# Handing out the experts of layer 0 unit by unit, with later stores and later transposes in the scan

## The chip, the cores and the metric

The kernel runs on one core of one Trainium2 chip. Five engines work side by side: TensorE (PE, matmuls; PEld is its weight load), VectorE (DVE), ScalarE (ACT), GpSimd (POOL) and SyncE (SP, which issues nearly all DMAs here). Each takes its instructions in the order of its own queue. The metric is the device time of one execution in microseconds (us). Before the change it is 3905.21 us, the median of three runs (3901.26 to 3909.09).

## The reference: what is computed

Input `x` has 16 sequences of 512 tokens, 128 wide; everything is float32. Two layers follow each other; each normalises `x` and adds an attention branch and a feed-forward branch to it.

```python
xn = _layernorm(x)
x = x + _L0_attn_ref(xn, ...) + _L0_ffn_ref(xn, ...)
xn = _layernorm(x)
x = x + _L1_attn_ref(xn, ...) + _L1_ffn_ref(xn, ...)
```

- `_L0_attn_ref` is a memory that is trained while it reads: a scan over 8 chunks of 64 tokens (all sequences at once). Each step projects keys and values, runs a two-layer network on the keys, takes the gradient of a squared error by hand, clips it and updates the weights. Then every token is read out through the final memory.
- `_L0_ffn_ref` is a convolution over time, attention with 16 heads of 8 (no mask), a layer norm, then a dense mixture of 8 experts: every token goes through every expert (128 to 512 to 128), weighted by a softmax gate, and another layer norm.
- `_L1_attn_ref` is causal attention with 16 heads, a convolution over its result, and a second causal attention with the queries that come out of it.
- `_L1_ffn_ref` picks 8 of 32 experts for each token, with room for 128 tokens in each expert, gathers the tokens, runs the experts and scatters the results.

## The kernel before

**Turns.** The program is not written engine by engine. Work is a set of Python generators ("stages"), and class `Turns` (L269 to L300) steps all that are live once a turn, in order of a priority: 0 the maxima (`tops`, which calls `largest`), 1 the weighted values (`back`, which calls `weighted`), 2 to 5 everything else, 6 the experts of layer 0 (`experts0`, which calls `ffn(b)` for one sequence after the other). PE's instructions keep exactly the order in which the generators write them; the other engines' queues are ordered by a scheduler. `idle(n)` lets n turns pass, `after(...)` waits for a mark, `room()` for a free buffer of `work`. A stage is given with the turn at which it may begin; those of layer 1 begin at fixed turns, from `t0 = 480` in steps of 44 for each sequence (L1456 to L1470), once the scan is over.

**Attention.** For one group of heads, `largest` (L370) writes scores into the PSUM tile `s1` (tag `p1`, one buffer), 1024 columns in a turn, and VectorE takes their maximum into `nm`: one reduction at L395 without a mask, at L387 with one (two instructions), or L394 and L395 for the narrow ones. The width of the causal scores runs through 512, 384, 256 and 128 columns. `weighted` (L419) writes the scores again, transposed, into `s2` (tag `p2`, one buffer); ScalarE takes the exponential into `e` (L466); with a mask POOL clears the upper triangle (L470). The sums over values, `pc`, follow eight heads a turn (up to four in a group at once), in turns in which `tail` (L444) puts "values" among the locks.

**Experts of layer 0.** `ffn(b)` (L526) has 64 units for a sequence: `first(i)` multiplies 128 of the 512 hidden columns of one expert (`phe`, L579) and lets ScalarE take ReLU (L581); `second(i)` multiplies back into `pye` (L591) and, after each fourth, scales by the gate on ScalarE (L598) and adds on POOL (L599). How many units a turn gets is an account. `load_ns` sums an estimate of PE's work in the turn; `credit` grows by `TURN` (2750) less that, up to 4000, and each unit costs 1000. With `pools["pairs"]` true only pairs are handed out, and in a turn with "values" none unless more than three would be:

```python
            credit[0] = min(credit[0] + TURN - load_ns[0], 4000)
            more = int(max(credit[0] + 500, 0) // 1000)
            if pools["pairs"]:
                more = more // 2 * 2 if "values" not in locks or more > 3 else 0
```

`turn4` (L240) writes four transposes and adds 900 to `load_ns` and `array_ns`. `fill` (L194) adds an unused matmul at a turn's end when the experts have been away for more than two turns and `array_ns` is under `ARRAY` (860).

**The scan** (`scan`, L762) runs beside layer 0's attention. A step's keys are transposed into `kT`, `hidden(q)` multiplies and takes SiLU (ScalarE `sg` L848, VectorE `h` L851, POOL `ds` L853 to L855), `hidden_turned` transposes `h` to `hT`, `gradient` multiplies it (`py`) and works out the error; `timed` (L754) gives each part the turn of the step at which it starts (L923 to L928). After eight steps `readout(b)` runs for each sequence and stores `y` (L1034).

**Stores on SP.** SP's queue takes DMAs in order and each waits there for its data. POOL's rows are stored at L1034 (`y` of the readout), L1116 (`x1` after `post0`'s layer norm), L1170 (`x2` in `middle`) and L1279 (`x2` in `last`). The same queue carries the loads of queries and keys (L364), of expert weights (L512, L516) and the maxima's way through memory (L412, L416).

## Time and profile before

| what | before |
|---|---|
| median of three runs | 3905.21 us |
| the profiled execution | 3907.05 us |
| its span | 3905.3 us |
| granted clock of TensorE, mean | 0.961 |
| turns written | 1275 |
| SP's waits for POOL at the stores L1034, L1170, L1116 | 146.6, 115.6, 105.6 us |

The span runs from the first instruction to the last. A row of instructions in the trace has start and duration in us, engine, line and operation, and what it writes and reads; in brackets the idle time before it and what ended it. `xN` is the number of instructions merged. A PE row is the matmul itself; `PEld` rows are weight loads, which overlap with it. A row of a table of windows has the stretch and its length, then for PE, PEld, DVE, ACT and POOL the busy time in us with the number of instructions, then the granted clock of TensorE (1.00 is full speed), the share of the DMA engines and GB/s.

### The profile page before, as it was taken

To read this page: it belongs to the slowest core of one execution; us is meant where nothing else is said; L and a number is where in the kernel's file an instruction comes from. 1 tells how busy PE (TensorE), PEld (TensorE's weight loads), DVE (VectorE), ACT (ScalarE), POOL (GpSimd) and SP (SyncE) were. 2 spreads that over 40 slices of the span, in tenths; PEclk is the share of its full clock that TensorE was granted. 3 is DMA by queue.
4 is the path that set the end of the run, shared out by engine and by line. 5 is a ranking of instruction groups with operands and counts; after the bars stand their busy time and mean duration, and the time that the engine had idled before them with its cause. 6 is when DMAs were issued, how large, how long until landed. Compare 5 with 4: busy or idle time off the path is not lost.

```text
span 3905.3 us, 61944 instructions
## 1 busy us (share of the span) xinstructions
PE 3452.3 (88%) x22265; PEld 1887.3 (48%) x22265; DVE 2325.2 (60%) x5027; ACT 2156.1 (55%) x3687; POOL 1578.2 (40%) x2522
## 2 busy tenths in 40 slices
PE   5999789889889899999998998899999999987877
PEld 2445445445444444555555555555555555533343
DVE  5666556565665555554565666566656666677762
ACT  1555555556566677665555565555555555543443
POOL 5432433344232555324244334433443344333664
PEclk7999899999999999999999999999999999997999
DMA  4222212222222233423443434343434434333343
GB/s 159 65 65 73 64 48 79 71 65 67 81 66 86 85 105 95 149 76 96 128 110 92 122 111 120 95 114 109 121 90 118 113 105 106 105 95 84 85 92 84
DMA packets 289940, 370.52 MB, mean 95 GB/s; under 512 B 46008, under 2 KB 141408, under 8 KB 289248
## 3 DMA queue, kind: packets, MB, share of 16 engines
q1 hardware_dynamic: 282464, 359.73, 32.1%
q0 software_dynamic: 7168, 6.82, 1.1%
q8 instruction: 177, 2.90, 0.3%
q14 instruction: 131, 1.07, 0.1%
HBM read 236.59 MB, written 133.25 MB: 95 GB/s over the span
## 4 chain that ended last, share of the span: by engine, by line
PE 67%; DVE 15%; POOL 6%; ACT 5%; issue 4%; DMA 3%; SPq 1%; POOLq 0%; ACTq 0%; DVEq 0%
PE s L192 17%; PE pye L591 12%; PE pc L192 11%; PE phe L192 11%; DVE nm L395 6%; DVE s L387 3%; PE tp L244 2%; DVE s L394 2%; PE pgr L192 2%; ACT e L466 2%; PE tpc L244 1%; PE pq L192 1%; PE pcv L192 1%; PE pj L192 1%; ACT sq L258 1%
## 5 line engine op out<-in xcount | busy, mean ns | idle before, releaser
L466 ACT ACTIVATE e<-s 128x1024 f32<-128x1024 f32 (+1 forms) x1216 | 1190.9, 979 | 697.0 <-PE s L192 616.6
L395 DVE TENSOR_REDUCE nm<-s 128x2 f32<-128x1024 f32 (+1 forms) x704 | 861.4, 1224 | 645.3 <-PE s L192 638.0
L387 DVE CUSTOM_DVE_ANT_0 s<-s,sb_const 128x512 f32<-128x512 f32 (+1 forms) x1024 | 646.7, 632 | 531.2 <-PE s L192 513.5
L470 POOL TENSOR_SCALAR_AFFINE_SELECT e<-e 128x128 f32<-128x128 f32 (+2 forms) x1408 | 468.8, 369 | 999.5 <-ACT e L466 997.2
L192 PE MATMUL s<-kx,qx 64*128 64x512 f32 (+3 forms) x3072 | 623.7, 432 | 274.3 <-DVE nm L395 145.1
L192 PEld LDWEIGHTS s<-kx,qx 64*128 64x128 f32 x3072 | 276.2, 188 | 913.1 <-issue 338.0
L192 PE MATMUL pc<-e,vp 128*32 128x512 f32 (+3 forms) x6144 | 658.9, 518 | 33.4 <-POOL e L470 33.2
L591 PEld LDWEIGHTS pye<-ew,hTe 128*128 128x128 f32 x4096 | 509.9, 193 | 148.1 <-issue 135.5
L581 ACT ACTIVATE hTe<-phe,sb_cols 128x512 f32<-128x512 f32 x512 | 354.0, 691 | 403.0 <-PE phe L192 401.2
L591 PE MATMUL pye<-ew,hTe 128*128 128x128 f32 x4096 | 575.5, 284 | 0.7 <-DVE vp L345 0.7
L192 PE MATMUL phe<-x1T,ew 128*128 128x512 f32 x1024 | 535.3, 607 | 3.2 <-DVE pr L545 1.0
L192 PE MATMUL s<-qx,kx 64*128 64x512 f32 (+3 forms) x3072 | 508.9, 356 | 31.5 <-ACT e L466 26.9
L192 PEld LDWEIGHTS s<-qx,kx 64*128 64x128 f32 x3072 | 288.1, 189 | 69.7 <-ACT e L466 56.0
L394 DVE TENSOR_TENSOR s<-s,sb_const 128x512 f32<-128x512 f32 (+1 forms) x192 | 168.4, 877 | 244.5 <-PE s L192 244.0
L599 POOL TENSOR_TENSOR ac<-ac,y 128x512 f32<-128x512 f32 x128 | 165.0, 1289 | 338.7 <-ACT y L598 337.9
L192 PEld LDWEIGHTS pc<-e,vp 128*32 128x32 f32 x6144 | 153.4, 111 | 275.9 <-issue 184.7
L598 ACT ACTIVATE y<-pye,pr 128x128 f32<-128x128 f32 x512 | 146.8, 368 | 40.7 <-PE pye L591 36.3
L192 PEld LDWEIGHTS phe<-x1T,ew 128*128 128x128 f32 x1024 | 158.9, 195 | 19.6 <-issue 10.4
L387 DVE DVE_READ_ACCUMULATOR2_ANT nm<- 128x1 f32 x1024 | 144.5, 141 | 0.0
L199 PE MATMUL fill<-sb_pb,sb_const 128*128 128x512 f32 (+2 forms) x236 | 118.4, 590 | 10.3 <-DMA sb_pb<-in_pb 10.2
L205 POOL TENSOR_SCALAR rs_t<-ss 128x4 f32<-128x4 f32 (+1 forms) x56 | 12.5, 223 | 245.5 <-ACT sq L258 244.5
L966 POOL TENSOR_TENSOR cl<-cl,phalf 128x1 f32<-128x1 f32 x8 | 4.5, 568 | 172.9 <-ACT cl L965 172.9
(291 smaller groups left out, 3885.5 us busy)
## 6 DMA issues: line engine op xcount, KB each, us to landing
ew<-in_ew SPq DMA_DIRECT2D x256, 256.0 KB
kx<-rk SPq DMA_DIRECT2D x192, 256.0 KB
qx<-rq SPq DMA_DIRECT2D x128, 256.0 KB
rq<-hi SPq DMA_DIRECT2D x64, 256.0 KB
rq<-lo SPq DMA_DIRECT2D x64, 256.0 KB
rk<-hi SPq DMA_DIRECT2D x64, 256.0 KB
rk<-lo SPq DMA_DIRECT2D x64, 256.0 KB
qx<-r SPq DMA_DIRECT2D x64, 256.0 KB
```

The lines of the kernel that those rows point to most:

```text
L192: nc.tensor.matmul(o, lhsT=lhsT, rhs=rhs, start=start, stop=stop)
L199: nc.tensor.matmul(o[:, 0:n], lhsT=ident, rhs=cell[0][:, 0:n], start=True, stop=True)
L244: nc.tensor.transpose(tp[:, t * P : (t + 1) * P], src(t), ident)
L387: newest[0] = nc.vector.tensor_tensor_reduce(out=sv[:, r, 0, :], in0=sv[:, r, 0, :], in1=row["caus"][:, S - n :], scale=1.0, scalar=-BIG, ...
L394: nc.vector.tensor_tensor(dg, dg, bc(bc(row["caus"][:, S - P :], 1, per), 1, 2), ALU.add)
L395: newest[0] = nc.vector.tensor_reduce(nm[:, qt, :, t : t + per], sv, AX.X, ALU.max)
L466: nc.scalar.activation(e[:, :, 0 : per * n], s[:, :, 0 : per * n], AF.Exp, scale=SCALE)
L470: cleared[0] = nc.gpsimd.affine_select(out=ev[:, r, :, 0:P], in_=ev[:, r, :, 0:P], pattern=[[0, per], [1, P]], compare_op=ALU.is_ge, fill= ...
L581: nc.scalar.activation(hs[i], ph, AF.Relu, bias=col("fb", i))
L591: nc.tensor.matmul(pye[0][:, t, :], lhsT=h[:, t * P : (t + 1) * P], rhs=w2[e][:, f, :], start=(f == 0 and t == 0), stop=(f == 3), skip_gro ...
L598: nc.scalar.mul(y[:, t, :], pye[0][:, t, :], pr[:, t, e : e + 1])
L599: nc.gpsimd.tensor_tensor(ac, ac, y, ALU.add)
```

## The change

Six things are done.

1. `pools["pairs"]` is false in both places where it was true. Units go out singly, in turns with "values" too.
2. Each turn of `largest` sets `look_ns` to a time for its maxima, by width and mask. If the account is not under -2000, the turn gets at least enough units that `load_ns` comes near `look_ns`. It is set to zero at each turn's end.
3. `turn4` adds 600 instead of 900.
4. In the scan, `hidden_turned` and `gradient` start one turn later in each step.
5. The stores of the readout, of `post0` and of `middle` come three, four and three turns after POOL's last instruction. In `post0` and `middle` these idle turns stood behind the store before.
6. The store in `last` comes two turns after POOL's addition.

```diff
-        load_ns[0] += 900
-        array_ns[0] += 900
+        load_ns[0] += 600
+        array_ns[0] += 600
...
-                load_ns[0] = 0.0
+                load_ns[0] = look_ns[0] = 0.0
...
+            look_ns[0] = {S: 2050, 3 * P: 1800, 2 * P: 2450, P: 3000}[n] if causal else 1750
...
+            if credit[0] > -2000:
+
+                more = max(more, int((look_ns[0] - load_ns[0] - 400) / 1000 + 0.7))
...
-    pools.update(ps=ps, p1=1, p2=1, work=3, weights=[att], heads=4, pairs=True)
+    pools.update(ps=ps, p1=1, p2=1, work=3, weights=[att], heads=4, pairs=False)
...
-                *[(4 + 2 * q + i, hidden_turned(q, i)) for q in range(2) for i in range(2)],
-                (7, gradient(0)), (9, gradient(1)),
+                *[(5 + 2 * q + i, hidden_turned(q, i)) for q in range(2) for i in range(2)],
+                (8, gradient(0)), (10, gradient(1)),
...
             nc.gpsimd.tensor_tensor(y, y, xb, ALU.add)
+            yield from idle(3)
             nc.sync.dma_start(acc_b[b], y)
...
         yield from layernorm(x1, x1, row["g1"], row["b1n"])
+        yield from idle(4)
         nc.sync.dma_start(x1d[0, b], flat(x1))
-        yield from idle(4)
...
-    pools["pairs"] = True
+    pools["pairs"] = False
...
         nc.gpsimd.tensor_tensor(x2, x2, xa, ALU.add)
+        yield from idle(3)
         nc.sync.dma_start(acc_b[b], x2)
-        yield from idle(3)
...
             nc.gpsimd.tensor_tensor(x2, x2, xo, ALU.add)
+            yield from idle(2)
             nc.sync.dma_start(acc_b[b], x2)
```

More of the change, by code (lines that the diff above doesn't have):

```diff
@@ L180, in flat @@
         return ap.rearrange("p t d -> p (t d)")
-    load_ns, array_ns, at_ffn = [0.0], [0.0], [-9]
+    load_ns, look_ns, array_ns, at_ffn = [0.0], [0.0], [0.0], [-9]
     def mm(o, lhsT, rhs, start=True, stop=True):
```

## The prediction

> **What bounds the kernel.** I read the page's busy shares first, then its slices, then who waits for whom, stage by stage.

> ```profile
> PE 3452.3 (88%) x22265; PEld 1887.3 (48%) x22265; DVE 2325.2 (60%) x5027; ACT 2156.1 (55%) x3687; POOL 1578.2 (40%) x2522
> PE   5999789889889899999998998899999999987877
> PEclk7999899999999999999999999999999999997999
> ```

> TensorE (PE) is busy 88%, no other engine over 60%, so its work sets the time, except that 453 us of the span are PE idle. The question is who ends those waits. First the scan's stretch (110 to 1570 us), then the causal stretch with experts (1640 to 3260 us), each for the matmuls (PE) and for their weight loads (PEld):

> ```profile
> PE s L192 <- DVE nm L395: 52.7, 60, 3.7
> PE s L192 <- DMA kx<-rk: 14.5, 2, 12.9
> PE tp L244 <- DVE h L851: 6.3, 4, 2.4
> PEld s L192 <- DVE nm L395: 167.0, 167, 4.6
> ...
> PEld s L192 <- DVE nm L387: 147.6, 196, 1.9
> ```

> The columns are total us, times, longest. The score matmul `s` of the maxima waits for VectorE to finish the maximum of the turn before: `p1` has one buffer, so PE may not write the next scores earlier. So a turn has two lower bounds: PE's own work W, and a floor D, first scores to maxima read. I cut the trace's matmuls at each turn's first matmul, by the order that the turn loop writes. Turns without other work show D: 1.82 us for the full maxima without mask, and in layer 1 2.17, 1.82, 2.65 and 3.30 us for widths 512, 384, 256 and 128. W is summed from start-to-start times. An expert unit is about 0.92 us, as here (pye to phe 0.97, phe to the next s 0.96):

> ```profile
> 2403.87 1.14 PE L591 MATMUL pye<-ew,hTe 128*128 128x128 f32 x8
> 2404.84 1.02 PE L192 MATMUL phe<-x1T,ew 128*128 128x512 f32 x2
> 2405.80 0.50 PE L192 MATMUL s<-kx,qx 64*128 64x512 f32 x2
> ```

> The longer of W and D, turn by turn, gives 1533 us for turns 520 to 1050; the trace has 1588, a ratio of 1.036. The rule holds there. For turns 60 to 492 (scan beside layer 0) it gives 1276 where the trace has 1402: 126 us are waits on chains of the scan and on DMAs.

> **The change, part by part.** All sums are against the profiled execution: 3907.05 us with a span of 3905.3. The median of the three runs, 3905.21, is the same within 0.05%.

> *Units one by one, in value turns too, and the bound from the maxima.* Before, in turns 520 to 1050, 253 turns have no unit, 213 two, 64 four. Of the empty ones 180 carry values and last 2.51 us at a W of 1.98; the 73 others last 2.63 at 1.78. Two units last 2.96 at a W of 2.81, four 4.76 at 4.62. The loss, D over W, is in the empty turns: 144 us of 530 turns (1533 less a W of 1389). Following the changed code's loop: 110 empty turns (mean of the longer bound 2.59), 73 with one unit and no values (2.66), 89 with one and values (2.82), 194 with two and no values (2.79), 30 with two and values (3.51), 33 with three (3.54), one of 4.79: 1498 us, of which 1417 are W (28 more because more units are done). Times 1.036: 1552, so **-36**. Ends: -116 (all floors gone: 1417 + 55) and +2: the 128 groups of ScalarE multiplications behind pye (L598, 1.14 us for four at 2405.04) come in more turns ahead of an exponential, and 0.3 us each gives 38 back. I take -36, nearest the turns measured.

> *A transpose counted 600 instead of 900.* Four transposes are 4 x 0.109 us start to start, so either is high. Seven sets per batch of 44 turns give 2100 ns of credit, 2.1 units: the last unit falls in turn 1050 instead of 1104. Turns 1050 to 1105 took 161.8 us. Without experts they go as turns 1105 to 1165 do, 2.53 each: 55 x 2.53 = 139, **-23**; turns 492 to 520 by the rule -2. [...] These windows start after the last expert:

> ```profile
> 3259.00:3418.00 159.00, 144.30 (x1071) 84.55 (x1070) 100.69 (x261) 91.41 (x144) 67.70 (x141) 0.99 0.39 107
> 3418.00:3470.00 52.00, 42.28 (x302) 21.16 (x298) 39.63 (x110) 24.15 (x31) 20.84 (x52) 0.90 0.34 103
> 3470.00:3520.00 50.00, 41.97 (x280) 18.49 (x280) 33.82 (x90) 21.51 (x26) 14.55 (x42) 0.97 0.39 97
> ```

> The clock (third from the end) goes from 0.99 to 0.90. [...]

> *More units during the scan.* Turns 60 to 492 now do 276 units, not 236: W up by 36, the longer bound from 1276 to 1288, since idle time takes most of it: **+12** (ends 0 and +36).

> *Stores later on SP's queue.* One stall shows what they do:

> ```profile
> 443.12 0.50 PE L192 MATMUL s<-qx,kx 64*128 64x512 f32 x2
> ...
> 453.89 0.32 SPq L1116 DMA_DIRECT2D x1d<-x  x1
> 454.39 0.32 SPq L364 DMA_DIRECT2D kx<-rk  x1
> ...
> 457.55 0.76 PE L192 MATMUL s<-kx,qx 64*128 64x512 f32 x1 [12.93 <-DMA kx<-rk]
> ...
> 461.00 2.07 PE L591 MATMUL pye<-ew,hTe 128*128 128x128 f32 x8
> ```

> The store of `x1` stands in SP until POOL's layer norm is done; the keys behind it land late, and PE stands for 13 us. It then runs cold: pye 2.07 instead of 1.14. That turn and the next are 12.5 and 5.0 over their bounds. [...] With four idle turns (13 us) first, the keys go ahead; POOL is next, and the longest store wait was 16.2 (L1116, 105.6 us in 11 waits). The other stores (L1034 146.6, L1170 115.6 us of SP waits) hold nothing that PE waits for beyond some 10 us of DMA waits in layer 1. **-18** (ends 0 and -27). Nothing needs a moved store soon: its readers wait for marks set later.

> *The scan's transposes and gradients a turn later.* PE waits for `h` (L851) at transposes and neighbours 6.3 + 3.9 + 2.4 + 1.7, and for `hT` 5.8: 20 in all. A turn of about 3 us covers most: **-12** (ends -20 and +10). Each of eight steps gets longer; `scan` ends in turn 492 instead of 486. The layer 1 work is dated by turn and absorbs most, but the last attention slips two turns (1275 turns to 1277): 2 x 2.94 = **+6**.

> *POOL bursts.* A layer norm of post0 takes 7 us of POOL (446.33 to 453.87). At 684.8 one, with the scan's keys and `ds`, held ScalarE's `sg`, and the exponential behind it cost PE 8.1 us. By the turn loop post0 and the hidden stage met once before and meet two or three times after (turns 172 to 177, 210 to 218, 338 to 343): **+10** (0 to +20).

> *Fills*: 53 more (170 for 117), nearly all in the first 60 turns or after the experts, where PE waits anyway: 0 (-5 to +10).

> Sum: -36 -23 -2 +12 -18 -12 +6 +10 = **-63**: a span of 3842, 3843 us by the median.

> **Rivals.**
> - *More is won in the scan.* If half of the 126 us of waits there go, instead of the 30 I count, it is 33 more, with more evened floors about 3800. For: most start at a transpose or a store that is moved. Against: several are POOL's own chain, which stays.
> - *Given back.* ScalarE's multiplications and ReLUs, now in value turns, delay the exponentials and cost the 38; with two more POOL meetings (+20) that leaves -5: 3900. For: the exponential is the other single-buffered wait (`p2`). Against: ScalarE is 55% busy.
> - *Slower.* In the scan's stretch experts fill the slack of the turns, so POOL's meeting with `ds` holds `sg`, then the exponential, then PE, each time some 10 us with the cold clock. It decides from eight such meetings over those counted (+80): 3922. For: 126 us of such waits already stand there. Against: only 14 post0 and 8 scan steps share these turns.
> - *The change does nothing*: excluded; empty turns fall from 864 of 1275 to 668 of 1277.

> **How the numbers follow.** Forecast 0.60 (own range 3815 to 3875), more won 0.14, given back 0.09, slower 0.17. The range 3795 to 3915 leaves a tail at each side. 0.2% (8 us) is about what a measurement here tells from no change. Faster by more: 0.60 and 0.14 and a fifth of the given back, 0.76; the same 0.06; slower 0.18.

> **What would show it.** Right: waits of `s` on `nm` in 1640 to 3260 us fall by a third; no 13 us gap behind L1116's store; the last pye some 200 us earlier (before: turn 1104, 3418 us); the stretch behind it at 2.5 us a turn. Wrong: the causal turns no shorter than 2.95 on average with `e` waits in place of `nm`; or the scan's stretch over 1420 us with `ds` and `sg` ahead of PE's gaps.

## The result, and the profile after

The changed kernel takes 3876.49 us (median of five runs, 3871.43 to 3883.21) against 3906.45 us of the kernel before on the same chip: 30 us less, ratio 0.9923 with a 95% interval of 0.9906 to 0.9940. I forecast 3843, which is 63 us less in span. The direction came as forecast; the size is under half. The time lies just outside the 3815 to 3875 that I gave the forecast itself, and inside the whole range of 3795 to 3915.

The page of the changed kernel, busy shares and slices:

```profile
span 3878.0 us, 62191 instructions
PE 3507.0 (90%) x22371; PEld 1934.8 (50%) x22371; DVE 2313.0 (60%) x5027; ACT 2158.5 (56%) x3687; POOL 1573.3 (41%) x2522
PE   6989999889989988989999999999999998888877
PEclk7999999999999999999999999999999999997998
```

PE idles 371 us of the span instead of 453. About 44 us of the 55 us that PE is busier are unused fill matmuls (342 rows of 563 ns for 236 rows before). The slices behind the last expert (from the 34th on) begin two slices earlier than before, and show 8 where the experts gave 9.

Who waits for whom in the changed kernel, the scan's stretch (110 to 1570 us) for PE and PEld, and the causal stretch with experts (1640 to 3240 us) for PEld; the columns are total us, times, longest:

```profile
PE s L192 <- DVE nm L397: 34.2, 35, 5.3
PE phe L192 <- DVE h L856: 12.6, 3, 7.4
PEld s L192 <- DVE nm L397: 103.0, 116, 5.5
...
PEld s L192 <- DVE nm L389: 69.5, 88, 1.9
PEld phe L192 <- issue: 47.6, 151, 0.7
```

The waits for the maxima fall from 52.7 to 34.2, from 167.0 to 103.0 and from 147.6 to 69.5 us. Two waits are new or grew. An expert's `phe` waits for the scan's `h`, and in the causal stretch the weight load of `phe` loses 47.6 us in 151 places to "issue", where before it lost 6.5 us in 19.

I cut the trace after the change at the same turns as before. "Rule" is the sum of the longer of PE's work and the floor of the maxima, with the durations of the prediction; "over" is what the trace has beyond it. The differences are those of the two profiled executions, whose spans are 27 us apart.

| turns | before: us, over | after: us, over | difference | forecast |
|---|---|---|---|---|
| 0 to 60 | 176.3, 38.5 | 172.7, 36.8 | -3.6 | 0 |
| 60 to 492 (scan) | 1401.6, 125.7 | 1401.4, 113.3 | -0.2 | -8 |
| 492 to 520 | 80.5, -0.7 | 79.0, 0.3 | -1.5 | -2 |
| 520 to 1050 (causal, experts) | 1587.9, 55.0 | 1574.9, 76.5 | -13.0 | -36 |
| 1050 to 1105 | 161.8, 3.3 | 140.5, 11.1 | -21.3 | -23 |
| 1105 to the end | 474.5, 77.8 | 487.1, 84.2 | +12.6 | +6 |

Of the 36 us that are missing, 23 lie in turns 520 to 1050, 7.8 in the scan's stretch and 6.6 at the end; the others give 1.4 back.

### The profile page after: what moved, and what is told of

It reads as the page before. It is cut to its first block, busy times and chain, and to the rows that moved or that the text cites. A ratio compares the mean times of both kernels' runs of the same rounds, so it can differ in the third digit from the quotient of the medians.

```text
span 3878.0 us, 62191 instructions
## 1 busy us (share of the span) xinstructions
PE 3507.0 (90%) x22371; PEld 1934.8 (50%) x22371; DVE 2313.0 (60%) x5027; ACT 2158.5 (56%) x3687; POOL 1573.3 (41%) x2522
## 5 line engine op out<-in xcount | busy, mean ns | idle before, releaser
L192 PE MATMUL s<-kx,qx 64*128 64x512 f32 (+3 forms) x3072 | 623.9, 433 | 177.9 <-DVE nm L397 94.1
L192 PE MATMUL pc<-e,vp 128*32 128x512 f32 (+3 forms) x6144 | 652.5, 512 | 28.8 <-POOL e L472 28.5
L192 PEld LDWEIGHTS s<-kx,qx 64*128 64x128 f32 x3072 | 277.0, 190 | 700.0 <-issue 222.1
L593 PEld LDWEIGHTS pye<-ew,hTe 128*128 128x128 f32 x4096 | 520.3, 194 | 196.6 <-issue 181.4
L192 PE MATMUL phe<-x1T,ew 128*128 128x512 f32 x1024 | 559.8, 631 | 21.2 <-DVE h L856 12.6
L192 PE MATMUL s<-qx,kx 64*128 64x512 f32 (+3 forms) x3072 | 507.6, 356 | 25.6 <-ACT e L468 19.4
L192 PEld LDWEIGHTS s<-qx,kx 64*128 64x128 f32 x3072 | 289.7, 190 | 53.8 <-ACT e L468 37.8
L192 PEld LDWEIGHTS pc<-e,vp 128*32 128x32 f32 x6144 | 153.8, 111 | 268.5 <-issue 184.7
L192 PEld LDWEIGHTS phe<-x1T,ew 128*128 128x128 f32 x1024 | 160.0, 195 | 119.2 <-issue 87.2
L199 PE MATMUL fill<-sb_pb,sb_const 128*128 128x512 f32 (+2 forms) x342 | 162.3, 563 | 10.7 <-DMA zrow<-zero 10.2
L199 PEld LDWEIGHTS fill<-sb_pb,sb_const 128*128 128x128 f32 x342 | 57.3, 209 | 56.4 <-issue 41.6
```

The lines of the kernel that those rows point to most:

```text
L192: nc.tensor.matmul(o, lhsT=lhsT, rhs=rhs, start=start, stop=stop)
L199: nc.tensor.matmul(o[:, 0:n], lhsT=ident, rhs=cell[0][:, 0:n], start=True, stop=True)
L593: nc.tensor.matmul(pye[0][:, t, :], lhsT=h[:, t * P : (t + 1) * P], rhs=w2[e][:, f, :], start=(f == 0 and t == 0), stop=(f == 3), skip_gro ...
```

## Experiments

Each ran 4 to 17 times beside the kernel before; "ratio" is to it. Three theories of the gain are set against each other in what was expected: "turns" (it comes from turns in which the floor of the maxima is over PE's work), "early end" (it comes from counting transposes at 600, which ends the experts earlier) and "stalls" (single stalls of the scan's stretch come or go).

| run | what it is | median us | ratio, 95% interval |
|---|---|---|---|
| only_units | before, single units | 3837.84 | 0.9817, 0.9804 to 0.9831 |
| only_600 | before, transposes counted 600 | 3868.14 | 0.9908, 0.9895 to 0.9922 |
| only_stores | before, later stores | 3912.31 | 1.0005, 0.9998 to 1.0013 |
| only_scan | before, scan's turns later | 3874.98 | 0.9915, 0.9901 to 0.9928 |
| after_even | after, no lone unit beside values | 3890.29 | 0.9955, 0.9941 to 0.9969 |
| after_no_scan | after, scan's turns as before; computes wrong values | 3846.79 | 0.9852, 0.9838 to 0.9866 |
| after_no_600 | after, transposes counted 900 | 3854.62 | 0.9867, 0.9853 to 0.9882 |
| after_sg3 | after, three buffers for sg | 3841.23 | 0.9834, 0.9821 to 0.9847 |
| before_sg3 | before, three buffers for sg | 3873.31 | 0.9929, 0.9916 to 0.9942 |
| before_store_on_pool | before, L1116 on POOL's queue | 3894.02 | 0.9973, 0.9964 to 0.9983 |
| after_no_600_sg3 | both of the above, on after | 3821.00 | 0.9786, 0.9773 to 0.9799 |
| units_bound_sg3 | single units, bound, three buffers | 3794.50 | 0.9721, 0.9709 to 0.9734 |

The parts do not add: single units alone win 71 us, 600 alone 41, the scan's turns alone 34, and all together 30. Their stretches tell why (us, and over the rule in brackets):

| run | turns 60 to 492 | 520 to 1050 | 1050 to 1105 | 1105 to the end |
|---|---|---|---|---|
| before | 1402 (126) | 1588 (55) | 162 | 475 |
| after | 1401 (113) | 1575 (76) | 141 | 487 |
| only_units | 1361 (90) | 1563 (65) | 154 | 479 |
| only_600 | 1371 (79) | 1593 (57) | 146 | 476 |
| only_scan | 1344 (71) | 1602 (74) | 165 | 493 |
| after_even | 1394 (108) | 1592 (58) | 140 | 487 |
| after_no_scan | 1398 | 1553 | 137 | 476 |
| after_no_600 | 1362 (109) | 1573 (86) | 157 | 487 |
| after_sg3 | 1370 (82) | 1575 (76) | 138 | 483 |
| before_sg3 | 1373 (97) | 1584 (51) | 162 | 478 |
| after_no_600_sg3 | 1331 (77) | 1572 (85) | 159 | 486 |
| units_bound_sg3 | 1335 (72) | 1552 (61) | 154 | 478 |

### Single units alone

```diff
-    pools.update(ps=ps, p1=1, p2=1, work=3, weights=[att], heads=4, pairs=True)
+    pools.update(ps=ps, p1=1, p2=1, work=3, weights=[att], heads=4, pairs=False)
...
-    pools["pairs"] = True
+    pools["pairs"] = False
```

> The kernel before with single units alone (pairs off in both places; nothing else). Turns theory (the gain comes from turns in which the floor of the maxima is over TensorE's work): by the rule (longer of work and floor) turns 520 to 1050 fall from 1533 to 1498 and the whole by 50 us; less some 25 to 30 us for 114 turns in which a lone unit stands beside values at 0.27 us over the sum: 15 to 30 us faster, ratio 0.992 to 0.996, with turns 520 to 1050 about 10 to 15 us shorter. Early-end theory (the gain comes from counting transposes at 600, which ends the experts 54 turns earlier): within 8 us of before, since here they end only 15 turns earlier. Stalls theory (the gain is single stalls of the scan's stretch that come or go): turns 520 to 1050 unchanged, turns 60 to 492 off by 10 us or more either way.

It is 71 us faster, more than any theory had. Turns 520 to 1050 lose 25 us, where the turns theory gave 10 to 15 and the two others nothing or little. So evening out the units is what pays in the causal stretch. Another 41 us are in the scan's stretch, and 35 of them are not in the rule but over it (126 to 90): stalls, the third theory.

### Lone units beside values

In the changed kernel's trace, 89 turns of the causal stretch have one unit and values. They last 3.09 us where the rule had 2.82: 24 us in all. In `only_units` 102 such turns are 28 us over. Their median is 0.15 us over; no other kind with more than five turns has a median above 0.09. First a turn with values and no unit in the kernel before, then one with a lone `phe` in the changed kernel, PE's matmuls in order of time (start, duration):

```profile
2253.60 0.44 PE L192 MATMUL s<-kx,qx 64*128 64x384 f32 x2
2253.88 0.56 PE L192 MATMUL s<-qx,kx 64*128 64x128 f32 x8
2254.36 1.07 PE L192 MATMUL pc<-e,vp 128*32 128x256 f32 x16
2255.42 0.44 PE L192 MATMUL s<-kx,qx 64*128 64x384 f32 x2
```

```profile
2317.58 0.44 PE L192 MATMUL s<-kx,qx 64*128 64x384 f32 x2
2317.86 0.56 PE L192 MATMUL s<-qx,kx 64*128 64x128 f32 x8
2318.35 1.07 PE L192 MATMUL pc<-e,vp 128*32 128x256 f32 x16
2319.35 1.13 PE L192 MATMUL phe<-x1T,ew 128*128 128x512 f32 x2
2320.41 0.44 PE L192 MATMUL s<-kx,qx 64*128 64x384 f32 x2
```

and the weight load of that `phe`, among the PEld rows:

```profile
2319.35 0.30 PEld L192 LDWEIGHTS phe<-x1T,ew 128*128 128x128 f32 x2 [0.41 <-issue]
```

The first turn is 1.82 us, the floor, and hides what is in it: 0.28 and 0.49 us of scores and 1.00 of `pc`, 1.77 together, for which the rule had 1.60. The second shows it, because `phe` starts only 1.00 us after `pc`. Its weights are loaded only as it starts (0.41 us of waiting), and the unit takes 1.06 us start to start, not the 0.97 and 0.96 of the pair that the prediction shows. The sum is 2.83 instead of 2.51. The extra of the unit is not the work of `pc` alone: in the causal stretch of this trace the median of a `phe` is 1.06 us between `pc` and `s`, but 0.96 with a `pye` behind it, after `pc` and after `s` alike. A lone unit pays on both sides. The test takes these units away and leaves the rest of the change:

```diff
                 more = max(more, int((look_ns[0] - load_ns[0] - 400) / 1000 + 0.7))
+            if "values" in locks:
+                more = more // 2 * 2
```

> The changed kernel with units in turns with values in even numbers only (none lone there, 90 before). By the rule alone 36 us slower in turns 520 to 1050 (1534 for 1498). If a lone unit after values costs 0.27 us over the sum, as the 89 turns of the changed kernel's trace show (3.09 us at a longer bound of 2.82), 24 of it come back: turns 520 to 1050 at 1580 to 1595 against 1575. If the excess is not the lone unit's, 1600 to 1615.

Turns 520 to 1050 take 1592 us, inside the first range: 17 us more, where the rule alone says 36, and 58 over the rule instead of 76. So 19 of the 24 us come back, and the lone unit does cost about this much. The test is not clean: the same edit leaves 44 turns with two units and values instead of 30, and they last 4.26 us on average instead of 3.69. The lone unit still pays: without it more turns are left to the floor.

### Stores, and where SP puts them

```diff
         yield from layernorm(x1, x1, row["g1"], row["b1n"])
+        yield from idle(4)
         nc.sync.dma_start(x1d[0, b], flat(x1))
-        yield from idle(4)
```

(and the three other stores as in the change)

> The kernel before with the later stores alone; TensorE's order is the same but for none or few places. The stall of 12.5 + 5.0 us behind the store of x1 at turn 144 goes: 10 to 20 us faster, ratio 0.995 to 0.9975, all of it in turns 60 to 492, if the store is its cause. If the layer norm on POOL itself held TensorE, or another DMA waits next, turn 144 keeps over 8 us and the time stays within 8 us.

Nothing comes of it: 1.0005, and turn 144 takes 14.4 us as before. SP's order says why. In the two traces the first 483 of SP's 1946 DMAs, which hold the stores of `x1` of the first ten sequences, stand in the same order; the eleventh store moves by one place. Only PE keeps the order of the turns; the scheduler had put the store there already, presumably behind POOL's expected end, and `idle` hardly moves it. That the store is the cause of the stall is shown by taking it out of SP:

```diff
-        nc.sync.dma_start(x1d[0, b], flat(x1))
+        nc.gpsimd.dma_start(x1d[0, b], flat(x1))
```

> The kernel before with the store of x1 after post0's layer norm (L1116) issued from POOL's own queue instead of SP's. If the keys of turn 144 are late because the store stands before them in SP, that turn falls from 12.5 us over the rule to under 4 and turns 60 to 492 get 10 to 20 us shorter, less some 16 us for 16 stores issued by POOL at about 1 us each beside its other work: the whole 0 to 20 us faster. If POOL's burst itself is what the keys wait for, turn 144 keeps over 8 us.

Turn 144 has no stall, and the keys are issued before POOL's norm begins:

```profile
440.49 0.41 SPq L364 DMA_DIRECT2D kx<-rk  x1
...
444.94 0.50 PE L192 MATMUL s<-kx,qx 64*128 64x512 f32 x1 [1.26 <-DMA kx<-rk]
...
446.68 4.16 POOL L229 TENSOR_SCALAR x<-x,ln_mv,ln_rs 128x128 f32<-128x128 f32 x4
```

The whole is 10 us faster; turns 214 and 215 still stall, 11 and 5 over.

### POOL's products and ScalarE's buffers

The changed kernel's worst turns in the scan's stretch are 219 (13.0 us over the rule), 342 (9.6), 93 (8.1) and 178 (5.8). Turn 219, all engines in order of time:

```profile
692.19 2.34 POOL L811 TENSOR_TENSOR v<-k,v 128x1024 f32<-128x1024 f32 x1
694.49 1.26 POOL L859 TENSOR_TENSOR ds<-sg,ds 128x512 f32<-128x512 f32 x1
...
695.78 0.60 ACT L853 ACTIVATE sg<-pp 128x512 f32<-128x512 f32 x1 [7.29 <-POOL ds L859]
...
697.08 0.69 DVE L856 TENSOR_TENSOR h<-sg,pp 128x512 f32<-128x512 f32 x1 [7.64 <-ACT sg L854]
...
697.91 2.04 PE L192 MATMUL phe<-x1T,ew 128*128 128x512 f32 x2 [4.99 <-DVE h L856]
```

POOL is behind with the keys' `v`. So `ds` is late, ScalarE waits to overwrite `sg`, `h` is late, and the PSUM buffer that `pp` holds is not free for `phe`. Everything behind `sg` on ScalarE waits too: the exponential starts only at 696.95. One more buffer takes this wait away:

```diff
-                sg = s1.tile([P, 2, INTER], F32, tag="sg", bufs=2, name="sg")
+                sg = s1.tile([P, 2, INTER], F32, tag="sg", bufs=3, name="sg")
```

(and the same number at `junk` and `qT`, which share the tag)

> The changed kernel with three buffers instead of two for the scan's sg (tag sg, at L847 of the kernel before), so that ScalarE's sigmoid, and with it the exponentials queued behind it, waits one POOL product later. Stall theory (the changed kernel wins little because the turns 93, 178, 219 and 342 stand 5 to 13 us each behind POOL's ds): time over the rule in turns 60 to 492 falls from 113 to 85 or less, the whole by 15 to 35 us to 3840 to 3862; turns 520 to 1050 unchanged at 1575. Rival (the stalls come from POOL being late as such, and one more buffer only moves the wait to h or dyT): within 8 us of 3876.

The stretch goes from 1401 to 1370 us, 82 over, and the whole to 3841. ScalarE's waits in that stretch, first of the changed kernel, then with three buffers:

```profile
ACT e L468 <- PE s L192: 187.0, 156, 6.7
ACT hTe L583 <- PE phe L192: 69.0, 71, 2.7
ACT sg L853 <- POOL ds L859: 35.1, 10, 8.3
```

```profile
ACT e L468 <- PE s L192: 193.0, 162, 6.8
ACT hTe L583 <- PE phe L192: 68.8, 74, 2.5
ACT gT L711 <- PE pg L192: 33.9, 1, 33.9
```

The waits of `sg` for `ds` fall from 35.1 us to 5.5 (three waits, not in the rows shown). The stretch is 31 us shorter and the whole 35.

> The kernel before with three buffers for sg and nothing else; TensorE's order of work is unchanged. Stall theory: the stall of turns 214 and 215 (14 us over the rule, ScalarE's sg behind POOL's ds) goes, the one of turns 144 and 145 (17 us, keys behind the store of x1) stays: 12 to 30 us faster, 3877 to 3895; against it the changed kernel with the same buffers (3841) is then 36 to 54 us faster, nearer to my forecast of 63 than the 30 of the pair as given. Rival (three buffers help only the changed kernel's layout): within 8 us of before, so that the pair with three buffers differs by 60 or more.

The kernel before gains 31 us from the same buffer. Turn 214 falls from 12.2 us to 2.3, but turn 215 grows from 9.0 to 13.1, so part of this stall only moved a turn; 144 stays. The two kernels with three buffers are 32 us apart (3873.31 and 3841.23), or 35 when each is set against the kernel before that ran beside it; I had expected 36 to 54. So these stalls hold both alike, and explain little of why the change wins less than half of the forecast.

### Counting transposes at 600, and the scan's turns

```diff
-        load_ns[0] += 900
-        array_ns[0] += 900
+        load_ns[0] += 600
+        array_ns[0] += 600
```

> The kernel before with a set of four transposes counted 600 instead of 900, alone. Turns theory: the units come earlier (last unit in turn 1071 instead of 1104) but as pairs, and seven turns are added at the end (1282): by the rule 13 us slower (0 to 25), ratio 1.000 to 1.006. Early-end theory: 20 us faster or more, as turns 1050 to 1105 get shorter at no cost elsewhere. Stalls theory: anything within 20 us, decided in turns 60 to 492.

```diff
-                *[(4 + 2 * q + i, hidden_turned(q, i)) for q in range(2) for i in range(2)],
-                (7, gradient(0)), (9, gradient(1)),
+                *[(5 + 2 * q + i, hidden_turned(q, i)) for q in range(2) for i in range(2)],
+                (8, gradient(0)), (10, gradient(1)),
```

> The kernel before with the scan's transposes and gradients one turn later, alone. As predicted: TensorE's 20 us of waits for h and hT fall by 12, six turns come in at the end (1281): within 15 us of before, waits of transposes for h under 5 us. Stalls theory: the step's new place against POOL's layer norms decides; meetings show as turns of over 8 us in turns 60 to 492 and the ratio may be anywhere from 0.995 to 1.008.

Both were expected near zero by the turns theory and are 41 and 34 us faster. By the rule the first is 13 us slower. What falls is the time over the rule in the scan's stretch, 126 to 79 and to 71: both lay the scan out anew against POOL's work, and the stalls of turns 144 and 214 do not come up. Outside that stretch `only_scan` is slower than before (turns 520 to 1050 by 14 us, the end by 19).

On the changed kernel the scan's turns were also put back (`after_no_scan`). I expected 3886 to 3896 us if the later transposes were worth the 12 us of my forecast, and 3840 to 3880 if they only moved the meetings. It takes 3846.79. This kernel computes wrong values, for a reason that stays open, so its time is a sign and not a result. Its trace is plain all the same: the scan's stretch is 3 us shorter than in the changed kernel, turns 520 to 1050 are 22 us shorter and the end 11, and turn 144 stalls again (14.2 us), though the stores are later in it. Most of the 22 us, 15.7, lie in turns 520 to 564. There the changed kernel's turn 535 takes 10.9 us:

```profile
1711.17 1.26 POOL L601 TENSOR_TENSOR ac<-ac,y 128x512 f32<-128x512 f32 x1
1712.46 0.59 ACT L570 COPY y<-pb 128x512 f32<-128x512 f32 x1 [8.32 <-POOL ac L601]
1712.94 1.03 ACT L468 ACTIVATE e<-s 128x1024 f32<-128x1024 f32 x1
1714.02 0.80 PE L192 MATMUL s<-qx,kx 64*128 64x512 f32 x2 [6.64 <-ACT e L468]
1714.75 2.08 PE L593 MATMUL pye<-ew,hTe 128*128 128x128 f32 x8
```

The layer norm of `post0` and that of `middle` stand behind each other on POOL before this (1699.8 to 1711.2 us). ScalarE waits 8.3 us for POOL's `ac`, the exponential behind it is late, and PE waits for that. In `after_no_scan`, where `middle` can begin six turns earlier, no turn of the 44 takes over 6.0 us. In `after_no_600`, where the experts stand elsewhere, none takes over 5.7, so it takes both parts to make this stall.

The transposes were also counted 900 again on the changed kernel:

> The changed kernel with four transposes counted 900 again; the last unit falls in turn 1092 instead of 1050. Turns theory: units that are left for turns 1050 to 1092 fill turns that the maxima bound anyway, so by the rule 26 us are won (turns 60 to 492 1253 instead of 1288, 520 to 1050 1487 for 1498, 1050 to 1105 150 for 129): 3840 to 3862. Early-end theory: the 600 was worth some 20 us, as it was alone: 3890 to 3900.

Counting 900 again makes the changed kernel 22 us faster, as the turns theory had it: units that are left for turns 1050 to 1092 stand in turns that the maxima bound anyway, while those pulled forward go into the scan's stretch, where PE has the least room (1401 us there against 1362, for 16 us won in turns 1050 to 1105). So 600 won alone by the layout that it happened to bring, against the rule, and costs in company.

### The parts that pay

> The changed kernel with transposes counted 900 and three buffers for sg. If the two add (each was 22 and 35 us under the changed kernel), 3820, within 10 us; turns 60 to 492 at 1325 to 1340, with under 80 us over the rule.

3821.00: 55 us under the changed kernel, where the two alone sum to 57.

> The parts that paid, together: the kernel before with single units, the lower bound from the maxima and three buffers for sg; transposes counted 900, stores and the scan's turns as before. Turns and stalls theory: by the rule 67 us under before, less 25 for lone units beside values, 15 more for the stalls: 3815 to 3840, the lowest so far. If the gain of single units alone (3838) already was the absence of stalls, 3838 or above.

```profile
span 3794.9 us, 61994 instructions
PE 3453.5 (91%) x22281; PEld 1903.1 (50%) x22281; DVE 2329.1 (61%) x5027; ACT 2154.1 (57%) x3687; POOL 1573.6 (41%) x2522
```

3794.50 us, below every range that I gave, and 82 us under the changed kernel. It differs from the run before it by the scan's turns and the stores alone, and the stores alone were worth nothing: without them 26 us are won, 20 of them in turns 520 to 1050 and 8 at the end. In the kernels with later turns of the scan, layer 1's attention stands two turns or more later beside stages with fixed turns.

## Why the prediction was right or wrong

- **Floor of the maxima against PE's work: right.** The written turns came as counted (1533 to 1498 by the rule for turns 520 to 1050), and the waits on `nm` fell there by half.
- **The -36 for these turns: the step that failed; measured -13.** "Times 1.036: 1552" carried the 55 us that the old turns had over the rule to turns that the trace before did not have, and "absorbs most" put the scan's later end at nothing here. The time over the rule came out at 76. Two causes are seen in it. One unit and values, costed at 2.82, measured 3.09, 24 us in 89 turns: values hidden under the floor were priced too low, and a unit that follows them alone is not half of a pair. And the scan's later end has a price: at turn 535 two layer norms stand behind each other on POOL, some 8 us, which neither the kernel without the later turns nor the one without the 600 shows; without the later turns the stretch is 22 us shorter in `after_no_scan` and 20 in the pair with three buffers. The two do not add up to the 23 that are missing: `units_bound_sg3` has 97 lone units beside values, at 3.09 us too, and still takes the 1552 that I forecast. How the 23 divide stays open. The end that I put up for this edit (+2) blamed ScalarE's multiplications, but PE's waits for `e` here grew only from 3.6 to 8.1 us, and 6.6 of these are turn 535.
- **The sign of being wrong that I named came half true.** The causal turns last 2.97 us on average, over the 2.95 that I set, but the waits are not those for `e`. A slip in the reading before: 4.76 us for four units is the mean of 59 turns; the five with values took 6.46.
- **Earlier end of the experts: right in its place (-23, measured -21), wrong as a gain.** Turns 1050 to 1105 went as the turns after the experts did, clock and all:

```profile
3079.00:3238.00 159.00, 150.56 (x1090) 89.64 (x1089) 97.63 (x256) 93.28 (x149) 60.85 (x135) 0.98 0.39 106
3238.00:3290.00 52.00, 45.15 (x290) 19.93 (x290) 35.79 (x98) 22.27 (x30) 26.47 (x56) 0.90 0.27 73
```

  The clock falls from 0.98 to 0.90 behind the last expert, as it did before (there at 3418 us, where the second window of the prediction starts). The 2.53 a turn (139 us for these turns) came nearer to the measured 140.5 than the floors alone (an estimate: 2.23 a turn from 16 at 2.17, 16 at 1.82, 8 at 2.65 and 4 at 3.30 us, 123 us for 55). How much between them is clock is not shown: PE's own work already puts the rule at 129, and 11 are over it. And the bill for the units moved forward is higher than the +12 that I put against it: without the 600 the changed kernel is 22 us faster.
- **Stores: wrong (-18, measured +3 alone, no change within the noise).** The cause of the stall was read rightly, and PE did run slow behind it (the kernel before was granted a clock of 0.50 from 457 to 463 us). The step "with four idle turns (13 us) first, the keys go ahead" failed, since SP's order is not the order of the turns. In the changed kernel turn 144 has no stall because the scan stands elsewhere: with its old turns the stall is back.
- **Scan's turns (-12): wrong in company.** PE's waits of transposes for `h` went as forecast (0.9 us, against 6.3 before and 11.2 in `after_no_scan`), but others came in their place (`phe` for `h`, 12.6). Against `after_no_scan` the later turns are worth nothing in the scan's stretch (+3) and cost behind it.
- **POOL bursts (+10): the mechanism right, the size not.** Stalls stand at turns 178, 219 and 342, beside the three places that I named, but they cost 28 us. The stretch came out at -0.2 where the four terms gave -8.
- **Two turns at the end: +6, measured +12.6.** The turns are there (1277); the rest is over the rule, and in `after_no_scan`, with 1275 turns, this stretch is within 2 us of the kernel before.
- **Fills: 0, and they cost nothing that shows** (turns 0 to 60 are 3.6 us shorter).

Open: why turns 520 to 1050 are up to 20 us longer with the scan's turns later, beyond turn 535. In `only_scan` the long turns come at the same turn of each sequence (639, 683, 727 and so on, 6 to 9 us each); in the other pairs they do not, and which engine ends them was not tried. The lower bound from the maxima (`look_ns`) never ran alone. And which meetings a given layout of the scan brings was only seen afterwards: the time over the rule in its stretch ranged from 71 us (`only_scan`) to 130 (`only_stores`) with edits that should not have touched it.

## What to carry to other kernels

The length of a turn does not price an instruction hidden under another engine's floor (here 1.77 us of scores and `pc` under 1.82): before filling its slack, sum its parts from start-to-start rows, and price the first matmul of another shape behind it by itself (here a `phe` of 1.06 us behind `pc` and before `s`, where the pair had 0.96). Where only one engine keeps the written order, look at the built order of a queue before counting on a store that is written later. When edits do not add, cut the trace at the same points for each, and separate what a rule explains from stalls; then take away the stalls' cause (here one buffer), in both kernels. And run the change without each of its parts: here one part, expected to win 12 us, cost its company 26 in the last pair of runs.
